# A two-layer graph, state-space and expert-mixture kernel: where the counts, the chunk ends and the routing steps stand, how the second mixture is split, and how many buffers its gathers rotate through

## The chip, the cores and the metric

The kernel runs on one core of a Trainium2 chip. The metric is device time in microseconds (us) of one execution. Five engines each work through their own queue in order: TensorE (PE, with its weight loads shown as PEld), VectorE (DVE), ScalarE (ACT), GpSimd (POOL) and SyncE (SP, which here only issues DMAs). Plain DMAs are issued by SP. Indirect DMAs (gathers and scatters by a list of row numbers) are issued by POOL.

## The reference, cut to what matters

Two layers over 4096 tokens of 256 features. `adj` is 4096 x 4096 and sparse (each row holds about eight non-zero values besides its diagonal).

```
# layer 0
x = x + L0_gnn(layernorm(x), adj)      # relu(adj @ x @ gcn_w + gcn_b), layernorm, then a
                                       # selective scan (state 16, inner 512) along the tokens
x = x + L0_ffn(layernorm(x))           # 8 experts, top 2, gelu, hidden 512
# layer 1
x = x + L1_gnn(layernorm(x), adj, adj)
x = x + L1_ffn(layernorm(x))           # 6 experts, top 2, three 256x256 matrices each

def L1_gnn(h, adj, simlar):
    sim  = tanh(adj * simlar)
    filt = sim * (adj > 0)
    vals, idx = top_k(filt, 700)       # all of a row, if it has at most 700 entries
    nnz  = sum(filt != 0, axis=1)
    keep = arange(700) < nnz
    new_adj = zeros.at[rows, idx].set(where(keep, vals, 0))
    h2 = tanh(h @ W_proj + b_proj)
    return relu(new_adj @ (h2 @ W_gcn) + b_gcn)

def L1_ffn(f):
    rh = relu(f @ router_w1 + router_b1)
    p  = softmax(rh @ router_w2 + router_b2); top_w, top_i = top_k(p, 2)
    w  = softmax(top_w)
    return sum over the two chosen experts of w * expert(f)
```

## The kernel before, in words

Tokens are worked in 8 chunks of 512 (`CW`, `NC`); a chunk is 4 tiles of 128 rows (`TPC`). The stages follow one another in one program:

1. **Lead-in** (to the first scan). Eight layer norms of `x` into `gn` (outside any order written by hand), then inside `tc.manual_schedule`, where the order of the code is the order on PE, DVE, ACT and POOL, the generator `propagation(0)` (L832): for each half chunk of 256 columns it streams 8 tiles `at` of `adjT` (128 x 4 x 256, three buffers, loaded by SP) and multiplies them with `gn`. One half takes 33 `advance` steps. In between, the neighbour lists of the listed chunks (2, 4, 6) begin: `lists.pair(q)` (L528) loads two row blocks of `adj` in eight pieces, finds the eight largest of each 512 columns on DVE (L562, L563), and four more pieces sort and pack them. The first list's twelve pieces (`EARLY_LISTS`) stand on DVE before the chunk's bias `L909`, with which the chain to the first scan begins.
2. **Scan** of layer 0, eight chunks of 32 steps, paced by DVE.
3. **First mixture** (8 experts) in tiles of 256 rows, `expert_tiles` (L666), with the rest of the lists beside it.
4. **Features**: `Features` (L1721) for each chunk combines the expert outputs (`yg`), norms, transposes, projects and writes the rows of `gnd` that gathers read. Its tiles and those of the later routing rotate through `WORK` buffers of tag `fm`.
5. **Neighbour loop** (L1863 to L1890), also in an order written by hand, SP included. It has 80 iterations: the five dense chunks (0, 1, 3, 5, 7) by 16 tiles of `adjT`. Iteration `k` does, in this order: `source(k+3)` (three ACT passes over the tile, and on DVE the count of positive entries, L1814 or L1817), `fetch(k+5)` (SP), the running `Route.prepare` generators one step each, the running `table`, `taken.upto(int(PACE*(k-2)))`, and `product(k)`: eight matrix products on PE, shown as sixteen records of L1825. After a chunk's last product, `finish` (L1830) closes it: a count product on PE, its maximum, bias, relu and residual on DVE. A load waits until ACT and DVE are done with the tile that had its buffer (`AHEAD + 1` buffers), a source until PE is done with the `f` that had its buffer (`LEAD + 1`), so PE can be only some six iterations ahead of DVE.
   The listed chunks are not multiplied. `Listed` (L1667) has 216 slots (6 pairs of tiles by 36); for each, POOL gathers 128 rows of `gnd` into one of ten ring buffers (L1681), and DVE adds them, scaled, into `x3` (L1697), in the order of the slots; a buffer is gathered into again when DVE has used it. Six of the buffers are tiles of their own, four are the rows of `x3` of the last chunk, which must be given up (`retire`) six iterations before the end.
   `ROUTES` says at which iteration a finished chunk starts its routing for the second mixture (`Route.prepare`, L637): layer norm on DVE (with `rsqrt`, L93, by four Newton steps), four transposes per half on PE (L144), a hidden layer (L197), logits (L654), top-2 choice (`router`, L147), placing (`place`, L269) and one-hot rows (`one_hot`, L319). `Part.tables` (L343) turns the choices of the first `SPLIT` chunks into row lists for POOL and expert numbers for SP, in groups of 8 columns: DVE, ACT, then PE (L419).
6. **Second mixture**, in two lots of tiles: 27 for the first six chunks (`few[0]`), 11 for the last two. Beside the first lot's tiles, `also` (L1953) advances the routing and table of the remaining chunks; beside the second lot's, `to_out` combines the first lot's chunks and stores them. The last two chunks are combined at the very end. `combine` (L729) reads with three `yg` buffers, two of which one chunk needs.

A program prints the functions that the change touches:

## Time and profile before

Three runs of the kernel before took 2341.86, 2342.48 and 2334.57 us. The profiled execution took 2333.76 us, of which its span, from the first to the last instruction, is 2332.0. The stages, cut at the first scan, the first and last product of the neighbour loop, the first expert product of the second mixture and the last bias of its two lots:

| stage | from | to | length us | PE busy | DVE busy | POOL busy |
|---|---|---|---|---|---|---|
| lead-in | 0 | 147.8 | 147.8 | 134.1 | 88.9 | 14.2 |
| scan | 147.8 | 1245.0 | 1097.2 | 1035.9 | 1054.7 | 817.1 |
| first mixture | 1245.0 | 1559.0 | 314.0 | 280.2 | 197.4 | 141.4 |
| features | 1559.0 | 1662.7 | 103.7 | 77.0 | 51.9 | 11.3 |
| neighbour loop | 1662.7 | 2052.7 | 390.0 | 324.3 | 313.4 | 277.1 |
| to the second mixture | 2052.7 | 2059.5 | 6.8 | 2.5 | 6.6 | 4.6 |
| second mixture, first lot | 2059.5 | 2232.0 | 172.5 | 171.6 | 67.3 | 105.2 |
| second lot | 2232.0 | 2310.7 | 78.7 | 68.2 | 33.2 | 33.8 |
| last stores | 2310.7 | 2332.0 | 21.3 | 0.0 | 6.7 | 1.9 |

How to read it: times within a row overlap, since the engines work side by side. Where one engine's busy time comes near the length of the stage, it sets the stage's length; where none does, waits between engines do, and they have to be read from the views of waits and from the order of time. A gather's own time on POOL (about 1.3 us) is that of issuing it; the rows land later.

### The profile page before, as it was taken

To read this page: it belongs to the slowest core of one execution; us is meant where nothing else is said; L and a number is where in the kernel's file an instruction comes from. 1 tells how busy PE (TensorE), PEld (TensorE's weight loads), DVE (VectorE), ACT (ScalarE), POOL (GpSimd) and SP (SyncE) were. 2 spreads that over 40 slices of the span, in tenths; PEclk is the share of its full clock that TensorE was granted. 3 is DMA by queue.
4 is the path that set the end of the run, shared out by engine and by line. 5 is a ranking of instruction groups with operands and counts; after the bars stand their busy time and mean duration, and the time that the engine had idled before them with its cause. 6 is when DMAs were issued, how large, how long until landed. Compare 5 with 4: busy or idle time off the path is not lost. (4 is left out here: it accounts for less than half of the span.)

```text
span 2332.0 us, 28125 instructions
## 1 busy us (share of the span) xinstructions
PE 2093.7 (90%) x8229; PEld 1498.5 (64%) x8229; DVE 1820.0 (78%) x3229; ACT 1196.5 (51%) x2064; POOL 1406.7 (60%) x1054
## 2 busy tenths in 40 slices
PE   8999999999999999997896999968978978799995
PEld 7666665656666565654564787855767766677874
DVE  4869999999999999999997997125377988864243
ACT  4256657465665746567673324214667765623321
POOL 1047777787877778776763454521387676746652
PEclk9999999999999999998897999988989998899998
DMA  8579899999989999998975999743455454367896
GB/s 293 169 207 247 229 282 239 271 248 250 268 231 283 241 269 249 252 263 240 278 262 170 300 366 317 231 145 118 153 152 169 148 168 136 108 206 219 248 293 214
DMA packets 302677, 532.29 MB, mean 228 GB/s; under 512 B 31323, under 2 KB 170575, under 8 KB 301616
## 3 DMA queue, kind: packets, MB, share of 16 engines
q1 hardware_dynamic: 244720, 416.84, 55.9%
q0 software_dynamic: 57792, 113.54, 21.8%
q8 instruction: 69, 1.13, 0.2%
q14 instruction: 96, 0.79, 0.1%
HBM read 434.34 MB, written 49.02 MB: 207 GB/s over the span
## 5 line engine op out<-in xcount | busy, mean ns | idle before, releaser
L1315 POOL TENSOR_TENSOR db<-du,bb 128x1024 f32<-128x1024 f32 x256 | 607.2, 2372 | 311.1 <-DVE hc L1348 74.3
L1338 DVE TENSOR_TENSOR_SCAN db<-da,state,db 128x512 f32<-128x512 f32 x512 | 627.3, 1266 | 19.9 <-ACT da L1331 17.7
L844 PE MATMUL pt<-at,gn 128*128 128x256 f32 x2048 | 478.3, 386 | 14.3 <-ACT gn L129 9.0
L844 PEld LDWEIGHTS pt<-at,gn 128*128 128x128 f32 x2048 | 396.5, 194 | 135.2 <-issue 63.8
L1331 ACT ACTIVATE da<-dt,negA 128x512 f32<-128x512 f32 x512 | 346.1, 688 | 245.7 <-DVE db L1338 235.9
L1348 DVE TENSOR_TENSOR hc<-db,cb 128x1024 f32<-128x1024 f32 x256 | 328.0, 1281 | 18.2 <-issue 0.9
L1365 PE MATMUL psy<-hc,ident 128*128 128x512 f32 x560 | 291.9, 615 | 3.4 <-DMA hc<-hc 3.4
L1825 PE MATMUL pf<-gn,f 128*128 128x256 f32 x1280 | 293.9, 391 | 0.0
L1825 PEld LDWEIGHTS pf<-gn,f 128*128 128x128 f32 x1280 | 250.4, 197 | 38.8 <-issue 3.3
L1681 POOL DMA_INDIRECT ring<-gnd,ls_idx x134 | 172.2, 1285 | 91.0 <-DVE x L1697 41.5
L690 PE MATMUL ps_h<-xkT,wk 128*128 128x256 f32 x864 | 214.4, 390 | 13.3 <-DVE xkT L715 12.1
L675 PE MATMUL ps_y<-wk,hk 128*128 128x256 f32 x864 | 214.0, 384 | 0.3
L680 DVE TENSOR_TENSOR yk<-ps_y,bk 128x512 f32<-128x512 f32 x73 | 50.2, 687 | 199.0 <-PE ps_y L675 161.0
L1352 POOL DMA_DIRECT2D hc<-hc x232 | 201.9, 870 | 0.2
L690 PEld LDWEIGHTS ps_h<-xkT,wk 128*128 128x128 f32 x864 | 159.1, 193 | 51.4 <-DVE xkT L715 19.0
L675 PEld LDWEIGHTS ps_y<-wk,hk 128*128 128x128 f32 x864 | 162.0, 192 | 22.1 <-ACT hk L694 1.6
L1365 PEld LDWEIGHTS psy<-hc,ident 128*128 128x128 f32 x560 | 105.2, 194 | 84.0 <-issue 60.1
L960 PE MATMUL ps_xz<-hT,w_in 128*128 128x512 f32 x256 | 117.0, 600 | 14.1 <-ACT hT L944 7.5
L694 ACT ACTIVATE hk<-ps_h,d0r_b 128x256 f32<-128x256 f32 x104 | 48.9, 474 | 136.1 <-PE ps_h L690 136.1
L1809 ACT ACTIVATE f<-at 128x1024 f32<-128x1024 f32 x80 | 84.4, 1055 | 64.6 <-PE pf L1825 56.9
L1681 POOL DMA_INDIRECT x<-gnd,ls_idx x82 | 101.3, 1235 | 27.0 <-issue 11.9
L694 ACT ACTIVATE hk<-ps_h,d1ap_b 128x256 f32<-128x256 f32 x108 | 51.2, 474 | 128.0 <-PE ps_h L690 127.9
(392 smaller groups left out, 3067.9 us busy)
## 6 DMA issues: line engine op xcount, KB each, us to landing
at<-in_adjT_dram SPq DMA_DIRECT2D x208, 512.0 KB, 4.7
bb<-bcd SPq DMA_DIRECT2D x128, 512.0 KB, 5.6
cb<-bcd SPq DMA_DIRECT2D x128, 512.0 KB, 5.3
hc<-hc POOLq DMA_DIRECT2D x232, 256.0 KB, 6.3
wk<-in_L_ffn_W_dram SPq DMA_DIRECT2D x70, 512.0 KB, 5.8
wk<-in_L_ffn_expert_w_dram SPq DMA_DIRECT2D x114, 256.0 KB, 4.3
ls_at<-in_adj_dram SPq DMA_DIRECT2D x32, 512.0 KB, 8.4
hc<-in_adj_dram SPq DMA_DIRECT2D x16, 512.0 KB, 5.2
```

The lines of the kernel that those rows point to most:

```text
L675: nc.tensor.matmul(ps[:, j, :], hT[:, m, j * P:(j + 1) * P], w[:, m, :], start=(m == 0), stop=(m == kb_out - 1),)
L690: nc.tensor.matmul(ps[:, j, :], w[:, d, m * P:(m + 1) * P], xT[:, d, :], start=(d == 0), stop=(d == DB - 1),)
L844: nc.tensor.matmul(pt[:, k, :], xl[:, j, k * P:(k + 1) * P], at[:, jj, :], start=(j == 0 and k == 0), stop=(j == NT - 1 and k == DB - 1),)
L960: nc.tensor.matmul(ps, w_in[:, k, m * P:(m + 1) * P], self.hT[:, k, :], start=(k == 0), stop=(k == DB - 1),)
L1315: nc.gpsimd.tensor_tensor(self.db, self.f.du[self.half][:, self.mi:self.mi + 1, :].to_broadcast([P, 2, CW]), self.bb, ALU.mult,)
L1331: nc.scalar.activation(da, self.f.dt[self.half][:, self.mi, :], AF.Exp, scale=negA[:, self.m, n:n + 1])
L1338: nc.vector.tensor_tensor_scan(self.db[:, j, :], da, self.db[:, j, :], state[:, self.m, n:n + 1], ALU.mult, ALU.add,)
L1348: nc.vector.tensor_tensor(self.hc, self.db, self.cb, ALU.mult)
L1352: nc.gpsimd.dma_start(self.hc[:, 0, :], self.hc[:, 1, :], accum_op=ALU.add)
L1365: nc.tensor.matmul(f.psy[m], ident, self.hc[:, j, :], start=False, stop=(self.g == GS - 1 and j == last),)
L1681: nc.gpsimd.indirect_dma_start(out=to[:, :], out_offset=None, in_=gnd[:, :], in_offset=bass.IndirectOffsetOnAxis(ap=lists.idx[:, q, s:s + ...
L1825: nc.tensor.matmul(pf[:, t, :], f[:, jj, t * P:(t + 1) * P], gn[:, j, :], start=(j == 0 and t % 2 == 0), stop=(j == NT - 1 and t % 2 == 1),)
```

## The change

It has six parts, all but the last two of which reorder or move work.

- The count of chunk 0 is made in the lead-in, from the tiles `at` that `propagation(0)` loads anyway, with a count product on PE and two maxima on DVE for each half; the loop's `source` and `finish` leave it out for chunk 0. The pieces of the first list now alternate with the second half's steps.
- `finish` runs at the start of the next iteration; the count product stays at the chunk's end (`total`).
- The layer norm of a routing yields between its statistics and its root and has one more empty step before the transposes; placing is two steps; the table's PE products run one step after the DVE work they read.
- `SPLIT` 5 instead of 6: the first lot is 23 tiles for five chunks, the second 15 tiles for three, 38 in all as before. The table of the first lot starts at iteration 69 with one step each instead of 75 with two.
- The ring has twelve buffers (four of its own, the four rows of the last chunk, and the four of the last listed chunk, the latter until slot 132), then eight; all 216 slots are done inside the loop at `PACE` 2.85.
- `rsqrt` makes three Newton steps instead of four. `WORK` is 8.

```diff
-SPLIT = 6
+SPLIT = 5
-RING = 10
-WORK = 7
+RING = 4
+WORK = 8
-PACE = 2.8
-RETIRE = 6
-ROUTES = {17: 0, 29: 2, 33: 1, 49: 3, 55: 4, 64: 5}
-TABLES = 75
-SPARE = 2
+PACE = 2.85
+ROUTES = {17: 0, 29: 2, 33: 1, 49: 3, 55: 4}
+TABLES = 69
...
-        for i in range(4):
+        for i in range(3):
...
         if alone:
+            yield
             rsqrt(rs, mv[:, :, 1])
...
             nc.tensor.matmul(
                 tot[:, :(G + 1) * E], ones, oh.rearrange("p g e -> p e g"), start=True, stop=True
             )
+            yield
...
+            last = None
+            def add():
+                if last is not None:
+                    g0, eq = last
+                    for g in range(S):
+                        nc.tensor.matmul(
+                            ps[:, :2 * C], dp.lo[:, g0 + g, :], eq[:, :2, g, :],
+                            start=(g0 + g == 0), stop=(g0 + g == NG - 1),
+                        )
...
-                for g in range(S):
-                    nc.tensor.matmul(
...
+                add()
+                last = (g0, eq)
                 yield
+            add()
+            yield
...
-            for _ in layernorm_parts(self.source[:, c * TPC:(c + 1) * TPC, :], xn, alone=True):
+            norm = layernorm_parts(self.source[:, c * TPC:(c + 1) * TPC, :], xn, alone=True)
+            next(norm)
+            yield
+            for _ in norm:
                 pass
+            yield
             yield
...
-        def propagation(c):
+        def propagation(c, count=False):
...
                     at = ats.pop(0) if ats else adjacency(r0, j4)
+                    if count and j4 == 0:
+                        cnt = w2p.tile([P, 4, HW], BF16, name="cnt0", tag="db")
+                        nc.vector.tensor_scalar(cnt, at, 0.0, None, ALU.is_gt)
+                    elif count:
+                        nc.vector.scalar_tensor_tensor(cnt, at, 0.0, cnt, ALU.is_gt, ALU.add)
...
+                if count:
+                    pc = ps_y.tile([P, CW], F32, name="psy", tag="psy")
+                    for jj in range(4):
+                        nc.tensor.matmul(
+                            pc[:1, :HW], ones[:, :1], cnt[:, jj, :], start=(jj == 0), stop=(jj == 3)
+                        )
+                    h = (r0 // HW) % 2
+                    nc.vector.tensor_reduce(chalf[:, h:h + 1], pc[:1, :HW], AX.X, ALU.max)
...
-            advance(NT + 1)
-            fr.do_gcn(1)
             made = [lists.pair(q, w2p, "hc", 6, 3) for q in range(EARLY_PAIRS)]
             made = itertools.chain(*made)
-            for _ in range(EARLY_LISTS):
+            for _ in range(NT // 4):
+                advance(4)
+                next(made)
+            advance(1)
+            fr.do_gcn(1)
+            for _ in range(EARLY_LISTS - NT // 4):
                 next(made)
...
-        ring = [keep1.tile([P, D], F32, name=f"ring{i}") for i in range(RING - TPC)]
-        tail_ring = [x3[:, NT - TPC + t, :] for t in range(TPC)]
+        ring = [keep1.tile([P, D], F32, name=f"ring{i}") for i in range(RING)]
+        early_ring = [x3[:, t, :] for t in lists.tiles[-TPC:]]
+        ring += [x3[:, NT - TPC + t, :] for t in range(TPC)]
...
+                self.last = len(self.slots) - TPC // 2 * PAIR - 12
             def fetch(self):
+                if self.next >= self.last:
+                    self.free = [f for f in self.free if any(f is r for r in ring)]
...
-            if j2 == 0:
+            if c == 0:
+                pass
+            elif j2 == 0:
...
+                if ended is not None and k % H2 == 0:
+                    finish(*ended)
+                    ended = None
                 if k in ROUTES:
...
                 if k >= TABLES:
-                    for _ in range(2):
-                        next(table, None)
-                if k == len(seq) - RETIRE:
-                    taken.retire()
+                    next(table, None)
                 taken.upto(int(PACE * (k - 2)))
-                if k == len(seq) - 1 and taken.left():
-                    taken.upto(max(taken.left()) + 1)
                 product(k, pf)
                 if j2 == H2 - 1:
-                    finish(c, pf)
-        assert not routes
+                    ended = (c, pf, total(c) if c else None)
+            finish(*ended)
+        assert not routes and taken.done == len(taken.slots)
...
         def routing():
             for b in range(NC - SPLIT - 1, -1, -1):
-                while b == 0 and taken.done < len(taken.slots):
-                    yield
                 for n, _ in enumerate(late.prepare(b)):
-                    if n % 6 == 5:
+                    if n in (5, 9):
                         yield
                 yield
...
         def also(n):
-            taken.upto(taken.done + SPARE)
```

In the built program, the order on DVE in the lead-in shows where the counts fall: the first three of the first half stand between the statistics of chunks 1, 2 and 3 and the step that asks POOL for their roots, the next two among the last chunk's statistics, and in the second half one count precedes each of the eight list pieces, with the half's maximum ahead of the list's last four pieces. On SP, four of the list's loads now stand ahead of the second half's second tile, where before its first three tiles stood ahead of them.

More of the change, by code (lines that the diff above doesn't have):

```diff
@@ L76 @@
     cmax = const.tile([1, NC], F32, name="cmax")
+    chalf = const.tile([1, 2], F32, name="chalf")
     x1d = [dram.tile([CW, D], F32, name=f"x1d{c}") for c in range(NC)]
@@ L106, in rsqrt @@
             nc.vector.scalar_tensor_tensor(t, t, -0.5, y, ALU.mult, ALU.mult)
-            nc.vector.scalar_tensor_tensor(rs if i == 3 else y, t, 1.5, y, ALU.add, ALU.mult)
+            nc.vector.scalar_tensor_tensor(rs if i == 2 else y, t, 1.5, y, ALU.add, ALU.mult)
     def layernorm_parts(src, dst, scalar=False, alone=False):
@@ L267, in choose_parts, with place, place_parts @@
             )
-        def place(self, b, psum, tag, pool):
+        def place(self, *args):
+            for _ in self.place_parts(*args):
+                pass
+        def place_parts(self, b, psum, tag, pool):
             E, G, g0 = self.E, 2 * self.T[b], 2 * self.t0[b]
@@ L417, in tables @@
                 )
-                for g in range(S):
-                    nc.tensor.matmul(
-                        ps[:, :2 * C], dp.lo[:, g0 + g, :], eq[:, :2, g, :],
-                        start=(g0 + g == 0), stop=(g0 + g == NG - 1),
-                    )
+                add()
+                last = (g0, eq)
                 yield
+            add()
+            yield
             inv = tp.tile([P, 2, C], F32, name="tb_inv", bufs=1)
@@ L660, in prepare @@
             yield from dp.choose_parts(b, logits, self.bias_b, True, small)
+            place = dp.place_parts(b, self.psum, self.tags[2], small)
+            next(place)
             yield
-            dp.place(b, self.psum, self.tags[2], small)
+            for _ in place:
+                pass
             yield
@@ L851, in propagation @@
                 halves.append(pts)
+                if count:
[6 more added lines that the diff above has]
+                    nc.vector.tensor_reduce(chalf[:, h:h + 1], pc[:1, :HW], AX.X, ALU.max)
+                    if h == 1:
+                        nc.vector.tensor_tensor(
+                            cmax[:, c:c + 1], chalf[:, :1], chalf[:, 1:], ALU.max
+                        )
                 yield True
@@ L1403, in advance @@
                 return k
-            prop = propagation(0)
+            prop = propagation(0, True)
             advance(NT + 1)
@@ L1661 @@
         gnd = dram.tile([N, D], F32, name="gnd")
-        for t in ring + tail_ring:
+        for t in ring + early_ring:
             nc.gpsimd.memset(t, 0.0)
@@ L1672, in __init__ @@
                 self.slots = [(q, s) for q in range(lists.n) for s in range(PAIR)]
-                self.free, self.at, self.next, self.done = ring + tail_ring, {}, 0, 0
-                self.keep = True
+                self.free, self.at, self.next, self.done = early_ring + ring, {}, 0, 0
+                self.last = len(self.slots) - TPC // 2 * PAIR - 12
             def fetch(self):
+                if self.next >= self.last:
+                    self.free = [f for f in self.free if any(f is r for r in ring)]
                 while self.free and self.next < len(self.slots):
@@ L1707, in upto @@
                     self.done += 1
-                    if self.keep or any(buf is r for r in ring):
-                        self.free.append(buf)
+                    self.free.append(buf)
                     self.fetch()
-            def retire(self):
-                self.keep = False
-                self.free = [f for f in self.free if any(f is r for r in ring)]
-            def left(self):
-                return [g for g, f in self.at.items() if not any(f is r for r in ring)]
         taken = Listed()
@@ L1811, in source @@
             nc.scalar.activation(f, f, AF.Tanh)
-            if j2 == 0:
+            if c == 0:
+                pass
+            elif j2 == 0:
                 cnt = cnts[c] = tb.tile([P, 2, CW], BF16, name="cnt", bufs=2)
@@ L1828, in product, with total @@
                     )
-        def finish(c, pf):
+        def total(c):
             pc = ps_m.tile([P, CW], F32, name="pc", tag="m")
@@ L1834, in finish @@
                 nc.tensor.matmul(pc[:1], ones[:, :1], cnt[:, jj, :], start=(jj == 0), stop=(jj == 1))
-            nc.vector.tensor_reduce(cmax[:, c:c + 1], pc[:1], AX.X, ALU.max)
+            return pc
+        def finish(c, pf, pc):
+            if pc is not None:
+                nc.vector.tensor_reduce(cmax[:, c:c + 1], pc[:1], AX.X, ALU.max)
             rows = slice(c * TPC, (c + 1) * TPC)
@@ L1852 @@
         )
-        routes = {}
+        routes, ended = {}, None
         with tc.manual_schedule(engines={
```

## The prediction

> **What bounds the kernel now.** I read the windows by stage first, then PE's waits in the stage that the change concerns, then that stage in order of time, then its gathers, and last the two places where the change adds work: the lead-in and the end. The scan is DVE's (1054.7 of 1097.2 us) and the change doesn't touch it. In the neighbour loop, 390.0 us long, no engine is full:
>
> ```profile
> 1662.70:2052.70 390.00, 324.33 (x1470) 273.30 (x1469) 313.44 (x801) 260.76 (x269) 277.12 (x220) 0.91 0.50 151
> ...
> 2059.50:2232.00 172.50, 171.59 (x824) 140.18 (x825) 67.29 (x232) 57.28 (x122) 105.15 (x108) 0.99 0.78 235
> ```
>
> Columns: window, length, then busy time and count of PE, PEld, DVE, ACT and POOL, clock, DMA. The loop's PE has 324 us of work, DVE 313, POOL 277; the second line, the second mixture's first lot, is full on PE. What PE waits for, loop and transition:
>
> ```profile
> PE ps_tr L144 <- DVE xn_r L134: 51.1, 6, 14.8
> PE pf L419 <- ACT tb_eq L413: 14.6, 2, 10.7
> ...
> PE ps_xt L711 <- DVE cmax L1899: 4.3, 1, 4.3
> ```
>
> The six routings cost 51.1 us of waiting for their norms, the table 14.6. Nothing else holds PE up. But this tells who was late, not why. In order of time:
>
> ```profile
> 1718.53 7.17 PE L1825 MATMUL pf<-gn,f 128*128 128x256 f32 x32
> 1740.54 2.42 PE L144 MATMUL ps_tr<-ident,xn_r 128*128 128x128 f32 x8 [14.84 <-DVE xn_r L134]
> 1742.75 5.02 PE L1825 MATMUL pf<-gn,f 128*128 128x256 f32 x16
> ...
> 1749.32 3.62 PE L1825 MATMUL pf<-gn,f 128*128 128x256 f32 x16
> ```
>
> An iteration of PE starts 3.45 us after the last while nothing holds it (32 records take 7.17); after a long wait the next 16 take 5.02, not 3.62, at a granted clock of 0.57 in that stretch. PE reached the first routing 18 iterations in, while DVE still waited for gathers. They are POOL's:
>
> ```profile
> L1681 POOL DMA_INDIRECT ring<-gnd,ls_idx x134 | 172.2, 1285 | 91.0 <-DVE x L1697 41.5 <-DMA gnd<-gn 21.3 <-issue 16.8
> L1681 POOL DMA_INDIRECT x<-gnd,ls_idx x82 | 101.3, 1235 | 27.0 <-issue 11.9 <-DVE x L1697 7.8 <-DVE d1a_oh L175 1.8
> ...
> 1692.69 1.22 DVE L1817 SCALAR_TENSOR_TENSOR cnt<-at,cnt 128x1024 bf16<-128x1024 f32 x1
> ...
> 1692.88 1.90 POOL L1681 DMA_INDIRECT x<-gnd,ls_idx  x1 [0.30 <-DVE x L1697]
> ...
> 1699.10 1.00 POOL L1681 DMA_INDIRECT ring<-gnd,ls_idx  x1 [0.30 <-DVE x L1697]
> ```
>
> 216 gathers took 172.2 + 101.3 = 273.5 us. Each also has 0.30 us before it, whatever happens: 64.8. That is 338 us, 1.57 each. Idle beyond that, without the first wait of 21.3, is 91.0 + 27.0 - 21.3 - 64.8 = 31.9. From 1667.8 this gives 2038, and the last indeed starts at 2036.9. An iteration takes 2.8 slots, so POOL alone asks 4.4 us for it against PE's 3.45. **So the loop is paced by gathers, and PE's waits are where it meets that pace.**
>
> **The change, part by part.**
>
> *Neighbour loop.* DVE loses the counts of chunk 0 (0.70 + 15 x 1.22 = 19.0), one routing (norm 6.5, choice 4.3, placing 2.9, one-hot 1.2: 14.9, summed from its rows), a Newton step in five routings (5 x 3 x 0.165 = 2.5) and a sixth of the table (2.5): 39 of 313. PE loses one routing (transposes, hidden layer and logits, 5.2 us). POOL's 216 gathers all stay. Fifteen fewer counts may each free the 0.4 us by which a gather beside one is longer (gathers beside one last around 1.4, alone 1.00): -6. The 31.9 us of extra idle stand at routings and chunk ends, 12 of them between 1787 and 1827 (19 gathers in 40 us), where DVE waits for products or exponentials that are only just issued. With those steps apart, DVE lighter and twelve buffers until slot 132, I take 24 of the 32 as gone. The last gather then ends at about 2038 - 30 = 2008. What hangs on it: DVE adds it (landing 3 us, two additions, 1.0), closes the last chunk (0.7 + 2 x 0.7 + 1.2 = 3.3); POOL gathers the first expert rows (2 x 1.3, landing 3.6); PE transposes and DVE copies (2). First expert product about 11 us behind: 2019, where now it is 2059.5. The table no longer decides, as it ends at iteration 77. **-40.** Bounds: if the idle doesn't shrink and only the counts help, the last gather ends at 2032 and the gain is 16; if all idle goes and gathers fall to 1.15, 216 x 1.45 from 1667.8 ends at 1981 and the product starts at 1992, -67, which PE just allows (1662.7 + 80 x 3.45 + 5 routings at 8 = 1979).
>
> [...]
>
> *Lead-in, added.* Sixteen counts on DVE, 19 us, and eight small PE products. The chain to the first scan starts from DVE:
>
> ```profile
> 46.24 0.69 DVE L562 MAX8 hc<-hc 128x8 f32<-128x512 f32 x1 [4.75 <-DMA hc<-in_adj_dram]
> ...
> 71.46 1.99 PE L902 MATMUL ps_gcn<-gcn_w,pts 128*128 128x256 f32 x8 [0.68 <-ACT pts L850]
> ...
> 77.08 1.28 DVE L909 TENSOR_TENSOR h<-ps_gcn,gcn_b 128x512 f32<-128x512 f32 x2
> ```
>
> PE's product was ready at 73.5, the bias waited for twelve list pieces: eight of 2.79 us (4 x 0.68 and loads) and four, 8.5 us. With counts a piece takes 4.0 us. In its favour, the list's first loads go out some 4 us earlier (one tile ahead of them, not three). First half: counts 2 and 3 stand before a root (2 x 1.2), hidden by the 3 to 5 us that norms are ahead of PE; count 4 holds its tile from 26.1 to about 29.4, so a later load is late and PE by 2 to 3.5. Then pieces from 42 to 74, the half's maximum 75, the rest of the list 84: the bias at about 83.8. **+6.5** (bounds +2, if tiles aren't held, and +13, if the loads come no earlier either). All of the scan moves with it.
>
> *Features.* One more `fm` buffer. The loads of `yg` stand behind the store of `gnd` on SP and wait for that, not for a buffer, but for 0.6 us every second chunk: **-0.5** (0 to -3).
>
> *First lot.* A third routing, and a table of three groups, not two, go beside tiles that fill PE. Undisturbed tiles end 6.04 or 5.21 us apart, 5.87 on average; the eight from 2080.8 to 2137.8, with two routings and the table, take 57.0, 10 more than 8 x 5.87. **+5**, half of that (+3 to +9).
>
> *Second lot.* 38 tiles as before. Its eleven took 78.7 us, 14 above 11 x 5.87, with the six combined chunks whose loads and stores stand before the next weights on SP. Five instead of six: **-2** (0 to -3).
>
> *End.* Three chunks to combine, not two, with three `yg` buffers:
>
> ```profile
> 2314.77 6.56 SPq L738 DMA_DIRECT2D yg<-d1b_ys  x6
> 2318.59 1.67 DVE L745 SCALAR_TENSOR_TENSOR oc<-yg,d1b_wv,x 128x256 f32<-128x256 f32 x4 [3.80 <-DMA yg<-d1b_ys]
> ...
> 2324.53 1.67 DVE L745 SCALAR_TENSOR_TENSOR oc<-yg,d1b_wv,oc 128x256 f32<-128x256 f32 x4
> ```
>
> The third chunk's second load needs a buffer that DVE frees at 2326.2. Load 3.5, eight additions 3.3, store 3.3, and the 2.8 from the last landing to the end: 2339.5. **+7.5** (+4, if loads overlap, to +10).
>
> Sum: 6.5 - 0.5 - 40 + 5 - 2 + 7.5 = -23.5. From the profiled execution's 2333.8 this gives 2310. That execution lies 8 us under the median of the three runs (2341.9), which spread from 2334.6 to 2342.5; I add half of the distance: **2314 us**.
>
> **The rivals.**
>
> *Gathers no longer bind* (PE or DVE does, first product at about 1995, -64 instead of -40): 2290. For it: gathers last 1.00 with DVE quiet. Against: the list additions, which lengthen most gathers, all stay.
>
> *The idle only moves.* DVE's additions keep their bursts, after slot 132 eight buffers serve where ten did, and 22 to 32 us of idle stay: loop -16 to -24, and with +16.5 elsewhere 0 to -7.5. Time 2334. For it: 41.5 us of ring idle were ended by DVE's additions.
>
> *Eight buffers throttle the second half: slower.* From slot 132 to the last, before, 84 gathers took 151 us (1.79 each) with ten buffers or six. If the round trip of a buffer sets the pace, eight make it 2.24. Gather 132 starts at 1667.8 + 132 x 1.55 = 1872, the last ends at 2060, the first expert product is at 2071, 11.5 later than now. With +16.5 elsewhere: +28, 2366. It decides from a pace of 1.90, at which the whole change gives nothing, and is slower by 0.5% from 2.04. Against: a buffer's trip is 1.3 + 3 landing + at most one iteration of 4.4 and a closing chunk, some 10 to 12 us, and 8 x 1.57 = 12.6 just covers it.
>
> **How the numbers follow.** Measurements of this kernel tell about 0.5% (12 us) from no change. Forecast 0.58, nearly all of it faster; gathers don't bind 0.14; the idle moves 0.17, of which 0.03 is faster; throttled 0.11, of which 0.02 is within 0.5%. Faster 0.74, same 0.17, slower 0.09. The range 2284 to 2342 takes in the forecast's bounds, most of the second case and half of the first. The forecast's own is 2298 to 2330.
>
> **What will show it.** The 16-record groups of L1825 should start some 4 us apart nearly throughout, with PE's waits for `xn_r` under 15 us in all and none for `tb_eq` over 4; the last L1681 should start near 2007 plus the lead-in's shift of 6.5, with extra idle under 12; the chunk's bias in the lead-in should start near 84, the first scan near 154; the first lot's early tiles should be slower for three routings; from last bias to the end some 29 us. It is wrong if the last gather ends as late as now, if the bias in the lead-in is at 77 or at 90, or if the pace of gathers beyond slot 132 is over 1.8.

## The result and the profile after

Six runs of each kernel on one chip: 2306.9 us median after (2304.8 to 2309.1), 2334.6 before (2333.8 to 2342.5). The ratio is 0.9871, with a 95% interval of 0.9854 to 0.9888: 27.7 us faster. The profiled execution took 2307.5 us, its span is 2305.6. Cut where the stages were cut before, in us:

| stage | before | after | difference | predicted |
|---|---|---|---|---|
| lead-in, to the first scan | 147.8 | 158.7 | +10.9 | +6.5 |
| scan, first mixture, features | 1514.9 | 1514.7 | -0.2 | -0.5 |
| neighbour loop, and on to the first expert product | 396.8 | 347.4 | -49.4 | -40 |
| both lots of the second mixture, 38 tiles | 251.2 | 255.3 | +4.1 | +3 |
| from the last bias to the end | 21.3 | 29.5 | +8.2 | +7.5 |
| sum | 2332.0 | 2305.6 | -26.4 | -23.5 |

The time lies 7 us under the 2314 that were predicted, well inside the range, and each stage went in the direction that was said. Two terms are mis-sized, the loop's and the lead-in's, and the loop's reason, as the experiments show, was not the right one.

The windows of the lead-in and of the loop (length, busy time of PE, PEld, DVE, ACT and POOL, granted clock, DMA):

```profile
0.00:158.67 158.67, 139.25 (x542) 104.58 (x543) 106.67 (x321) 54.14 (x97) 14.21 (x26) 0.97 0.63 206
...
1673.35:2013.60 340.25, 312.66 (x1438) 264.89 (x1437) 286.31 (x721) 257.61 (x263) 263.54 (x219) 0.95 0.57 171
```

In the loop PE is now busy for 312.7 of 340 us, where it was 324.3 of 390. What it waits for there and in the transition:

```profile
PE ps_tr L144 <- DVE xn_r L134: 13.1, 4, 5.9
PE pf L417 <- ACT tb_eq L429: 9.4, 2, 9.1
PE ps_pl L285 <- DVE d1a_oh L177: 4.5, 2, 3.3
...
PE ps_xt L733 <- DVE cmax L1941: 1.5, 1, 1.5
```

The norms' 51.1 us have become 13.1, the table's 14.6 have become 9.4, and nearly all of that is one wait. The waits of the placing (`ps_pl`), 4.5 us, did not stand among the waits before. In order of time, at the first routing and at the table:

```profile
1745.07 2.37 PE L144 MATMUL ps_tr<-ident,xn_r 128*128 128x128 f32 x8 [2.49 <-DVE xn_r L134]
1747.23 4.75 PE L1864 MATMUL pf<-gn,f 128*128 128x256 f32 x16
...
1977.91 0.82 PE L417 MATMUL pf<-tb_eq,d_lo 128*128 128x100 bf16 x8 [9.13 <-ACT tb_eq L429]
1978.53 5.21 PE L1864 MATMUL pf<-gn,f 128*128 128x256 f32 x16
```

The first routing stops PE for 2.49 us, not 14.84. The sixteen records behind a stop still take 4.75 or 5.21 us instead of 3.62. The gathers:

```profile
L1726 POOL DMA_INDIRECT x<-gnd,ls_idx x128 | 151.2, 1181 | 60.6 <-DMA gnd<-gn 21.2 <-issue 12.8 <-DVE x L1742 11.3
L1726 POOL DMA_INDIRECT ring<-gnd,ls_idx x88 | 109.2, 1241 | 31.3 <-DVE x L1742 12.7 <-issue 9.8 <-DVE cnt L1856 2.1
```

They take 260.4 us (273.5 before). Idle beyond the 0.30 of each and the first wait of 21.2 is 60.6 + 31.3 - 21.2 - 64.8 = 5.9 us (31.9 before). From slot 132 on, with eight buffers, they follow each other every 1.65 us, from start to start (1.82 before, counted the same way). The last one starts at 2008.5. In the lead-in, one wait of DVE's counts, the bias and PE's next step of the chain to the scan:

```profile
49.68 1.22 DVE L866 SCALAR_TENSOR_TENSOR cnt<-at,cnt 128x1024 bf16<-128x1024 f32 x1 [2.45 <-DMA at<-in_adjT_dram]
...
86.04 1.28 DVE L948 TENSOR_TENSOR h<-ps_gcn,gcn_b 128x512 f32<-128x512 f32 x2
...
91.97 2.80 PE L976 MATMUL ps_turn<-ident,h 128*128 128x128 f32 x8 [5.73 <-ACT h L968]
```

The bias starts at 86.04 instead of 77.08, and PE, which had its own product ready at 78.5, now stops 5.73 us for what follows from it. At the end, the loads and the last additions:

```profile
2280.16 6.68 SPq L760 DMA_DIRECT2D yg<-d1b_ys  x6
...
2297.47 1.67 DVE L767 SCALAR_TENSOR_TENSOR oc<-yg,d1b_wv,oc 128x256 f32<-128x256 f32 x4 [1.62 <-DMA yg<-d1b_ys]
```

### The profile page after: what moved, and what is told of

It is laid out like the page before. It is cut to its first block, busy times and chain, and to the rows that moved or that the text cites. A ratio compares the mean times of both kernels' runs of the same rounds, so it can differ in the third digit from the quotient of the medians.

```text
span 2305.6 us, 28092 instructions
## 1 busy us (share of the span) xinstructions
PE 2087.7 (91%) x8235; PEld 1492.4 (65%) x8235; DVE 1813.0 (79%) x3207; ACT 1196.3 (52%) x2064; POOL 1397.9 (61%) x1056
## 5 line engine op out<-in xcount | busy, mean ns | idle before, releaser
L1864 PE MATMUL pf<-gn,f 128*128 128x256 f32 x1280 | 289.2, 387 | 0.0
L712 PEld LDWEIGHTS ps_h<-xkT,wk 128*128 128x128 f32 x864 | 160.5, 195 | 49.5 <-ACT hk L716 14.6
L1726 POOL DMA_INDIRECT x<-gnd,ls_idx x128 | 151.2, 1181 | 60.6 <-DMA gnd<-gn 21.2
L697 PEld LDWEIGHTS ps_y<-wk,hk 128*128 128x128 f32 x864 | 160.5, 190 | 21.3 <-ACT hk L716 1.4
L1404 PEld LDWEIGHTS psy<-hc,ident 128*128 128x128 f32 x560 | 105.4, 195 | 84.8 <-issue 60.6
L1726 POOL DMA_INDIRECT ring<-gnd,ls_idx x88 | 109.2, 1241 | 31.3 <-DVE x L1742 12.7
L1016 PE MATMUL ps_xz<-xc,dK 128*128 128x512 f32 x256 | 114.8, 592 | 0.0
L1846 ACT ACTIVATE f<-at 128x1024 f32<-128x1024 f32 x80 | 84.4, 1055 | 51.1 <-PE pf L1864 39.2
```

What stands on the lines that cost most here:

```text
L697: nc.tensor.matmul(ps[:, j, :], hT[:, m, j * P:(j + 1) * P], w[:, m, :], start=(m == 0), stop=(m == kb_out - 1),)
L712: nc.tensor.matmul(ps[:, j, :], w[:, d, m * P:(m + 1) * P], xT[:, d, :], start=(d == 0), stop=(d == DB - 1),)
L1404: nc.tensor.matmul(f.psy[m], ident, self.hc[:, j, :], start=False, stop=(self.g == GS - 1 and j == last),)
L1726: nc.gpsimd.indirect_dma_start(out=to[:, :], out_offset=None, in_=gnd[:, :], in_offset=bass.IndirectOffsetOnAxis(ap=lists.idx[:, q, s:s + ...
L1864: nc.tensor.matmul(pf[:, t, :], f[:, jj, t * P:(t + 1) * P], gn[:, j, :], start=(j == 0 and t % 2 == 0), stop=(j == NT - 1 and t % 2 == 1),)
```

## The experiments

Every kernel but one is the changed kernel, altered in one part or, in the last, in three; the other is the kernel before with fewer gathers. "Extra idle" is POOL's between gathers, beyond 0.30 each and the first wait. The ratio is to the kernel before, timed on the same chip, which gave 2336.5 us (first four rows of experiments), 2332.0 (next four), 2335.2 (next three) and 2361.9 (the last). Kernels timed on different chips are best compared by this ratio, in which 0.0010 is 2.3 us. The other columns are those of the one profiled execution.

| kernel | median us | ratio, 95% interval | first scan | loop | extra idle | last gather ends |
|---|---|---|---|---|---|---|
| before | 2334.6 | 1 | 147.8 | 390.0 | 31.9 | 2037.9 |
| after | 2306.9 | 0.9871, 0.9854 to 0.9888 | 158.7 | 340.2 | 5.9 | 2009.5 |
| counts back in the loop | 2300.9 | 0.9846, 0.9822 to 0.9870 | 150.0 | 343.2 | 5.9 | 2009.2 |
| all steps together | 2350.6 | 1.0069, 1.0042 to 1.0096 | 157.8 | 383.7 | 30.4 | 2040.6 |
| eight buffers | 2315.0 | 0.9919, 0.9888 to 0.9950 | 157.2 | 342.9 | 7.1 | 2011.1 |
| split at six | 2318.8 | 0.9928, 0.9905 to 0.9951 | 158.9 | 361.9 | 12.8 | 2018.3 |
| chunk ends at once | 2304.4 | 0.9876, 0.9842 to 0.9909 | 158.9 | 338.9 | 3.8 | 2007.3 |
| routing at once | 2324.1 | 0.9962, 0.9947 to 0.9977 | 158.6 | 356.6 | 14.4 | 2030.5 |
| after, 180 gathers | 2291.7 | 0.9816, 0.9793 to 0.9840 | 159.5 | 329.3 | 27.6 | 1995.3 |
| loads ahead, five buffers | 2300.9 | 0.9853, 0.9828 to 0.9878 | 159.5 | 339.9 | 7.1 | 2013.1 |
| before, 180 gathers | 2326.8 | 0.9962, 0.9944 to 0.9980 | 149.8 | 379.0 | 67.9 | 2032.4 |
| table at once | 2334.7 | 0.9990, 0.9973 to 1.0007 | 158.0 | 365.4 | 15.3 | 2028.5 |
| lists behind the bias | 2299.8 | 0.9849, 0.9818 to 0.9881 | 149.6 | 339.7 | 5.9 | 2003.3 |
| three edits combined | 2368.0 | 1.0033, 1.0011 to 1.0056 | 148.0 | 366.3 | 31.7 | 2032.1 |

**Do gathers pace the loop?** The central claim of the prediction, tried on the kernel before.

```
+                    if s % 6 == 5:
+                        self.at[self.next] = None
+                        self.next += 1
+                        continue
                     to = self.at[self.next] = self.free.pop(0)
...
-                    buf = self.at.pop(g)
+                    given = self.at.pop(g)
+                    buf = b_gcn_b if given is None else given
```

> The kernel before, with every sixth gather left out (180 instead of 216); the additions of those slots add a constant row, so DVE's work stays, and the rows of the listed chunks come out otherwise. The prediction said that gathers pace the neighbour loop of the kernel before (390 us) and that PE's waits are where it meets that pace. Theory G (that is so): 36 x 1.57 = 56 us less on POOL; the loop falls until PE's work and the sixth routing and table stop it, 340 to 355 us, kernel -35 to -50 us. Rival P (the routing's and the table's waits set the loop, each stalling PE while DVE does a whole norm, and POOL only follows): loop within 8 us of 390. In between (both near the bound, as the same cut in the changed kernel gave 10.9 us of 54): 365 to 380.

With some 56 us of POOL's work gone, the loop fell by 11.0 us and the kernel by 8.5. The window of the loop and two stops of PE in it, those of the first and the last routing:

```profile
1669.20:2048.16 378.96, 322.66 (x1470) 272.32 (x1469) 312.62 (x801) 260.79 (x269) 239.91 (x184) 0.93 0.49 149
```

```profile
1739.14 2.42 PE L144 MATMUL ps_tr<-ident,xn_r 128*128 128x128 f32 x8 [6.90 <-DVE xn_r L134]
...
1969.53 2.21 PE L144 MATMUL ps_tr<-ident,xn_r 128*128 128x128 f32 x8 [10.39 <-DVE xn_r L134]
```

POOL's extra idle is 67.9 us now, and the last gather ends only 12 us earlier against the loop's start. The first stop shrank from 14.84 to 6.90; there DVE had been waiting for the first gathers (21.4 us in the kernel before, from 1665 to 1741). The others are nearly as long as they were. The time from the start of the iteration before to the start of the iteration named, in us:

```
iteration        18     30     34     50     56     65     75     76
before        20.66  11.66  10.73  14.83  10.97  16.21  15.01  10.34
180 gathers   12.72  11.51  10.73  13.76  10.90  16.05  15.01  10.21
```

In both kernels 54 of the 79 distances are under 3.7 us, and in them PE's records follow one another without idle time. The loop before the change thus ran at PE's own pace but for 25 iterations: of the 113.8 us by which its distances exceed 3.45 each, 101.6 stand in 14 distances of over 6 us, at stops or right behind one. Of these stops only the first hung on gathers for more than about 1 us. Theory G's 340 to 355 falls. With 379.0 the loop ends at the edge of what was called in between (365 to 380), 3 us outside rival P's bound: rival P but for the first stop, which gives 7.9 of the 11.0 us.

**The same cut in the changed kernel.**

> The changed kernel with every sixth gather left out (180 gathers instead of 216); the additions of those slots add a constant row instead, so DVE has the same work, and the rows of the listed chunks come out otherwise. POOL has 1.206 + 0.30 us a gather now, 331 of the loop's 340 us. Theory G (POOL's gathers still set the loop's length): 36 x 1.5 = 54 us less on POOL, the loop falls until PE stops it (80 x 3.45 + 5 routings of 8 = 316, or somewhat more with its remaining waits): loop 316 to 326, kernel -14 to -24 us. Rival P (PE, DVE and their waits set the loop now, POOL is only nearly full): loop within 4 us of 340. Rival D (DVE's 288 additions and counts pace it): likewise within 4 us, with DVE waiting less for gathers but busy throughout.

The loop fell by 10.9 us, to 329.3, where theory G wanted 316 to 326 and rival P 340: between the two. The kernel's ratio fell by 0.0055, some 13 us, just short of the 14 that theory G wanted at least.

```profile
1676.43:2005.78 329.35, 309.88 (x1438) 263.03 (x1437) 285.88 (x721) 257.27 (x263) 240.24 (x188) 0.97 0.56 172
```

PE is busy for 310 of 329 us. The distances at iterations 20, 32 and 52, each with a stop in it, went from 8.26, 12.14 and 9.80 to 4.33, 7.34 and 7.93; the table's, at 71, stayed (13.37 and 13.25). After the change gathers still lengthen the remaining stops at routings, by 0.2 us for each microsecond taken off POOL, the same share as before the change.

**All steps together, then one kind at a time.** First norm, placing, chunk ends and the table's products all as before the change (and with them the steps in which the second mixture takes its late routings):

```
-            yield
             rsqrt(rs, mv[:, :, 1])
...
-            next(norm)
-            yield
             for _ in norm:
                 pass
-            yield
             yield
...
-                add()
                 last = (g0, eq)
+                add()
                 yield
-            add()
-            yield
...
-            place = dp.place_parts(b, self.psum, self.tags[2], small)
-            next(place)
             yield
-            for _ in place:
-                pass
+            dp.place(b, self.psum, self.tags[2], small)
...
-                    ended = (c, pf, total(c) if c else None)
+                    finish(c, pf, total(c) if c else None)
```

> The changed kernel with one part undone: layer norm, placing, chunk end and the table's products stand in one step again, as before the change (the placing keeps its halves, run one right behind the other). Theory G (what counts is the extra idle before gathers, 5.9 us now, 31.9 before the change; apart steps remove idle because DVE no longer stands waiting with additions behind it): PE waits for xn_r return to over 35 us, extra idle of gathers rises to 18 to 25, loop +12 to +19, kernel 2319 to 2326. Rival P (the waits of PE for the norms set the loop): five norms with 8.5 us each and the table's 14.6 come back in full, +40 us or more, 2347. Rival C (counts and buffers made the loop's gain, the steps none): within 4 us of the changed kernel.

The loop grew by 43.5 us, nearly all that the change had gained there; this is rival P's number. PE's waits:

```profile
PE ps_tr L143 <- DVE xn_r L133: 34.2, 5, 11.8
PE pf L416 <- ACT tb_eq L428: 27.5, 5, 12.1
```

The extra idle of the gathers came back as well, 30.4 us, though POOL had nothing else to do than in the changed kernel. In the two kernels with 180 gathers it is 67.9 and 27.6 us. The idle time follows mostly from what holds DVE and PE; cutting gathers adds to it.

Chunk ends alone (only the last two lines of the diff above and the call of `finish` behind it):

> The changed kernel with only the chunk's end undone: bias, relu and residual follow the chunk's last product in its own iteration again, so that DVE waits there for products only just issued. With all steps undone the loop grew by 43.5 us, of which the idle of gathers is 24.6. Theory G (each step that DVE waits on holds additions, and so gathers, up): five ends, each holding DVE by some 2 to 3 us more: extra idle 6 -> 14 to 20, loop +8 to +15. Rival R (the routing and table steps make all of it): loop within 3 us of 340. Rival E (the ends make most of it): loop +25 or more.

Loop 338.9, kernel 2304.4: no effect that can be told. Rival R holds. Routing alone (statistics, norm and placing):

> The changed kernel with only the routing undone: statistics, root and norm of a routing in one step, the transposes one step earlier, placing in one step; chunk ends and table as in the changed kernel. Theory G: DVE does a whole norm (6.5 us) in one stretch and waits in placing for a product just issued; additions stand behind it; extra idle 6 -> 15 to 22, PE waits for xn_r from 13 to over 30, loop +15 to +25. Rival E (the chunk ends make most of the 43.5): loop within 8 us of 340. Rival T (the table's products make it): loop within 8 us, in this run and in the one with only the chunk ends undone.

Loop +16.4, PE's waits for `xn_r` 33.7 us (13.1), extra idle 14.4 (5.9): about the sizes that theory G gave, which rival P of the run before gives too, so this run does not tell them apart. The table alone:

> The changed kernel with only the table's products undone: each group's products on PE stand in the step of the DVE and ACT work that they read. All steps undone cost the loop 43.5 us, routing alone 16.4, chunk ends alone -1.3. If the parts add, the table makes the remaining 28: PE's waits for tb_eq go from 9 to over 25 us, loop +18 to +28, kernel 2325 to 2335. Rival J (the parts need each other: with the routing undone the table starts late and meets the loop's end, by itself it costs little): tb_eq waits below 20, loop below +10.

Loop +25.1, as was said if the parts add: PE's waits at the table are 24.1 us for `tb_eq` and 3.8 more put down to a DVE addition, where rival J wanted less than 20 and a loop below +10. The three parts, 16.4 + 25.1 - 1.3 = 40.2, nearly add up to the 43.5. The table's first three groups:

```profile
1983.69 0.82 PE L417 MATMUL pf<-tb_eq,d_lo 128*128 128x100 bf16 x8 [12.60 <-ACT tb_eq L429]
1984.31 5.31 PE L1862 MATMUL pf<-gn,f 128*128 128x256 f32 x16
1993.46 0.52 PE L417 MATMUL pf<-tb_eq,d_lo 128*128 128x100 bf16 x8 [3.84 <-ACT tb_eq L429]
1993.82 5.37 PE L1862 MATMUL pf<-gn,f 128*128 128x256 f32 x16
2003.02 0.82 PE L417 MATMUL pf<-tb_eq,d_lo 128*128 128x100 bf16 x8 [3.84 <-DVE x L1740]
```

Groups come about 10 us apart, where an undisturbed iteration is 3.45. PE reaches each group's products before DVE and ACT have made what they read; the next iteration's records then run at 5.3 us, and the next group finds PE waiting again. One step apart, only the first group stops it.

**The counts of chunk 0 back in the loop**, and the lead-in's former order.

```
-            prop = propagation(0, True)
+            prop = propagation(0)
...
-            if c == 0:
-                pass
-            elif j2 == 0:
+            if j2 == 0:
```

> The changed kernel with one part undone: chunk 0 is counted in the neighbour loop again, and the lead-in has its former order (both halves, then the twelve list pieces). Theory G (POOL's gathers pace the loop, a count costs the loop only what it lengthens a gather and the idle it causes): the bias of the lead-in starts at 77 instead of 86, the first scan at 148 instead of 159 (-11), the 15 counts after the first lengthen gathers by 0.4 us each (+6) and idle grows by 2 to 4, so the loop grows by 8 to 10: -1 to -3 us against the changed kernel. Rival D (DVE's work paces the loop): all 19.0 us of counts come back in the loop, 2307 - 11 + 19 = +8 us. Rival N (the loop has slack there): the loop stays 340 us and the kernel gains the whole lead-in, -11 us.

The bias starts at 78.0 and the first scan at 150.0, 8.7 us earlier; the loop grew by 3.0, the gathers' time by 2.7 (263.2), the extra idle not at all. 19.0 us of DVE work thus cost the loop 3: not the 19 of rival D, less than the 8 to 10 of theory G and more than rival N's nothing. The stages between took 5.7 us more in this one profile, though nothing in them differs; the median is 6.0 us lower, as -8.7 and +3.0 give, and the two intervals overlap. By the two stages, moving these counts together with the list's new order was a loss of 5.7 us; the medians alone don't show it.

**Four list pieces behind the bias.**

```
-EARLY_LISTS = 12
+EARLY_LISTS = 8
```

> The changed kernel with eight list pieces ahead of the chunk's bias in the lead-in instead of twelve; the other four (8.5 us of DVE) follow with the second list's pieces, behind the statistics. Theory B (the bias waits for DVE, and the lead-in's 10.9 us are DVE's counts ahead of it, PE's wait for the turn and the low clock that follows it): bias at 77.5 instead of 86, PE's wait for ps_turn from 5.7 to below 3, first scan 4 to 8 us earlier, kernel -4 to -8 us. Rival W (PE's own order paces the lead-in, which is busy 141 of its 159 us): bias at 77.5 all the same, first scan within 2 us of 158.7, kernel within 2 us. Rival L (the four pieces are late behind the bias): first scan later than 160.

```profile
77.53 0.67 DVE L948 TENSOR_TENSOR h<-ps_gcn,gcn_b 128x512 f32<-128x512 f32 x1
```

```profile
86.03 1.04 PE L976 MATMUL ps_turn<-ident,h 128*128 128x128 f32 x8
```

The wait of 5.73 us is gone, the turn takes 1.04 us instead of 2.80, and the first scan starts at 149.6: 9.1 of the 10.9 us are back, with the counts still in the lead-in. What is left, 1.8 us, is no more than profiles with the same lead-in differ: the first scan of the kernel before starts at 147.8 and, with fewer gathers, at 149.8; that of the changed kernel and of the runs that leave its lead-in alone at 157.2 to 159.5. The bias came 8.5 us earlier, which is what the four pieces take on DVE. So theory B is right about what the bias waits for, and its 4 to 8 us are a little exceeded; the low clock behind PE's wait (0.77 from 90 to 105 us) had little part in it, as the account of the lead-in below shows. Moving four pieces behind the bias of the kernel before, which waited for DVE as well (PE ready at 73.5, the bias at 77.1), was not tried. Of the kernels that do the whole computation this one has the lowest median, 2299.8 us, and by the ratio (0.9849) it is level with the counts back in the loop (0.9846); its interval overlaps that of the changed kernel, so the gain is read from the stage.

**Eight buffers from the start.**

```
-        early_ring = [x3[:, t, :] for t in lists.tiles[-TPC:]]
+        early_ring = []
```

> The changed kernel without the four early buffers: eight buffers for all 216 gathers. From slot 132 on, where it has eight anyway, the changed kernel makes a gather every 1.65 us, before that every 1.47. Theory G (a buffer's trip of 10 to 12 us is just covered by eight): the first 132 slots take 0 to 0.1 us more each, 0 to +13 us, I take +5. Rival T (the trip of a buffer sets the pace with eight): the first 132 slots go at 1.65 or slower, +24 us and more; with the 2.24 of the scaled trip +100.

Loop +2.7, extra idle +1.1. The median, 2315.0, comes from runs that spread from 2307.4 to 2321.9, and its interval only touches the changed kernel's; the profiled one took 2307.9, so the slower ones left no trace that tells why. Rival T's +24 us fails on every run: the trip of a buffer does not set the pace. In the profiled execution the four early buffers bring 2.7 us; in the median the kernel without them is 8 us slower, and the cause of the difference is open.

**Six chunks in the first lot.**

```
-SPLIT = 5
+SPLIT = 6
-ROUTES = {17: 0, 29: 2, 33: 1, 49: 3, 55: 4}
-TABLES = 69
+ROUTES = {17: 0, 29: 2, 33: 1, 49: 3, 55: 4, 64: 5}
+TABLES = 75
...
-                    next(table, None)
+                    for _ in range(2):
+                        next(table, None)
```

> The changed kernel with the split undone: six chunks in the first lot, a sixth routing in the loop from iteration 64, the table from 75 on with two steps each (and seven buffers of tag fm, as the sixth chunk's rows take that room). Theory G (the end pays for the third chunk, the loop gains little by the split, since gathers pace it): the end is 8 us shorter (21 instead of 29.5), the first lot 5 shorter, the second 2 longer, the loop and transition longer by the sixth routing's share: PE 5.2 us and gathers held up by 3 to 8, transition 4: together 0 to +6 us, 2307 to 2313. Rival S (the split made much of the loop's gain, as the sixth routing and its table stand at the end of the loop where nothing covers them): loop and transition +30, less the 11 at the end: 2326 or more.

The loop is 21.7 us longer, with 16.3 us of waits for `tb_eq` and 19.0 for `xn_r`; from the last bias to the last addition the end is 7.4 shorter (15.7 against 23.1), the tiles take 2.9 less. The median is 11.9 us above the changed kernel, about midway between the theories. Loop and transition together are 20.5 us longer, so the split gains twice the 10.3 that it costs.

**Loads of the last combinations a tile ahead.**

```
-        yg = [pool.tile([P, TPC, D], F32, name="yg", **(tag or {"bufs": 3})) for _ in range(2)]
+        yg = [pool.tile([P, TPC, D], F32, name="yg", **(tag or {"bufs": 5})) for _ in range(2)]
...
+                while going:
+                    next(going.pop(), None)
                 if (n - few[0]) % 3 != 0 and ready:
-                    stores.append(to_out(dp1[0], ready.pop(0), op[0]))
+                    going.append(to_out(dp1[0], ready.pop(0), op[0]))
+                    next(going[0])
```

> The changed kernel with the last combinations altered: a chunk's two loads are issued one tile ahead of the additions that read them, five buffers for these loads instead of three, the sums written in place, and the last chunk stored in two parts. In the changed kernel the second lot has three slow tiles (11.25, 8.74 and 10.20 us where 6.04 is usual), in which DVE waits 5.27 us for a load just issued and PE's next copy stands behind it. Theory A (a load issued a step ahead takes the wait away): the three tiles lose 8 to 12 us together; the end, where the third chunk's second load waited for a buffer, loses 2 to 4: -10 to -16 us. Rival Q (what holds the tile up is the loads and stores ahead of the next weights on SP): the slow tiles stay, only the end gains: -2 to -4 us.

```profile
2189.22 0.48 DVE L769 SCALAR_TENSOR_TENSOR x<-yg,d1a_wv,x 128x256 f32<-128x256 f32 x1 [5.00 <-DMA yg<-d1a_ys]
```

The end is 3.9 us shorter (19.2), as both theories said; the second lot's slow tiles stayed (12.28, 10.00 and 8.24 us). But the wait itself was not tried: the loads were issued at 2185.1 and the first addition stood on DVE 4.1 us later, as in the changed kernel (2184.7 and 2188.7). This part has no order written by hand, and putting the load earlier in the code did not put the addition later on DVE.

**Three edits combined**: the lists behind the bias, five buffers with the last chunk in two parts, and the table's products two steps behind.

```
-EARLY_LISTS = 12
+EARLY_LISTS = 8
...
-            def add():
-                if last is not None:
-                    g0, eq = last
+            def add(most):
+                if len(last) > most:
+                    g0, eq = last.pop(0)
```

> The changed kernel with three edits that the runs so far speak for: eight list pieces ahead of the lead-in's bias (by itself 2299.8 us, -7), five buffers for the last combinations' loads with the sums written in place and the last chunk stored in two parts (the end 19.2 instead of 23.1 us from the last bias to the last addition, -4), and the first lot's table products two steps behind their DVE work instead of one (PE still waits 9.1 us there, once, in iteration 71). If the stops of PE set the loop and one more step hides most of the last: 9.1 -> below 5, loop 340 -> 335, kernel 2290 to 2295. If that wait is one for DVE's backlog, and not for a step too early, it moves with the products: loop 339 to 342, kernel 2295 to 2298.

It was timed on a chip on which the kernel before took 2361.9 us (2347.7 to 2368.6), some 26 more than elsewhere, and was 0.3% slower than that, so neither forecast came. The profiled execution, 2346.1 us, is the fastest of its twelve, 22 us under their median. In its profile one iteration of the loop took 36.1 us, its records 2.1 to 2.8 us apart, with a kind of PE wait that none of the other profiles shows, one in which PE waits for nothing that the profile names:

```profile
PE pf L1865 <- issue: 28.8, 20, 2.2
...
PE pf L417 <- ACT tb_eq L429: 3.5, 4, 1.7
```

The table's wait did fall from 9.1 to 1.7 at the longest, and without the 32.7 us by which that iteration exceeds the usual one the loop would be 333.6. But the long iteration also let the other engines catch up (the stop at iteration 20 is missing behind it), so 333.6 is no measurement. The two lots took 266.7 us, 11.4 more than in the changed kernel, so the loop is not the only slow part of this profile. Whether the long iteration belongs to this kernel or to that chip is open, and so is whether the combination is faster.

## Why the prediction held, and where its reasons did not

**What bounds the loop.** "So the loop is paced by gathers, and PE's waits are where it meets that pace" is the step that failed. Cutting a sixth of the gathers took 11.0 us off the 390, not 35 or more, and nearly 8 of them at the first stop. The loop is PE's own 80 iterations of 3.45 us, 276 us, and the rest, 114 us before and 64 after, is stops, the routing's products and the slower records behind a stop (5.02 us for sixteen before, 4.75 and 5.21 after, instead of 3.62). The stops stand where PE reads what DVE and ACT were only then told to make: norms and hot rows of the table. Putting those reads back beside what they read, with the same work on every engine, cost the loop 43.5 us. How much of a stop is that step's own work and how much is DVE's backlog was not separated. The lines shown with the prediction could not settle it. Distances of 3.45 us right up to a stop look like PE's own pace, but PE may be some six iterations ahead: a loop held to POOL's 4.4 us an iteration falls behind PE by 0.95 us in each, so PE could run some 28 iterations (6 x 4.4 / 0.95, an estimate from these numbers) before it is held, and the longest stretch between two stops is 18. Only taking gathers away told the two apart. POOL's 338 us were added up to nearly the loop's length and its idle time was taken for a cause, though its releaser was DVE. That the sum met the last gather was no evidence either: the additions are tied to the iterations by `PACE`, so the last gather comes near the loop's end whatever sets the pace.

Of the signs that were named, the groups some 4 us apart throughout did not come (54 of 79 distances are under 3.7 in the changed kernel as before), nor did the table's waits of at most 4 us (one is 9.1) or the first scan near 154 (158.7). The waits for `xn_r` (13.1, under 15), the extra idle (5.9, under 12), the pace behind slot 132 (1.65, under 1.8) and the end (29.5 for some 29) came as said; the last gather started at 2008.5, 5 us before the time named.

**The loop's -40.** It came out at -49.4. That the steps apart are what helps was among its reasons, but each part was priced by what it saved the gathers, so that the number lies within its bounds is in part luck: the gathers ended earlier because the stops went, not the other way round. Undone one by one, routing is worth 16.4 us, the table 25.1, the split 21.7, the counts 3.0, the buffers 2.7, the chunk ends nothing; the sum, 68.9, exceeds the 49.8 that the loop lost, so the parts overlap. That the table's step matters less where the table has more time, as with the split, would explain it but was not tried. The Newton step, `PACE` and the retiring of buffers were not undone by themselves. The prediction gave the counts 6 us (measured 2.7 of gathers' time), and the table and the split no number of their own beyond "the table no longer decides". The last gather ended 39 us earlier against the loop's start, not 30 (the gathers' own time fell by 13.0 us, where 6 were said, the extra idle by 26.0, where 24 were), and the first expert product followed 11.3 us behind it, where 11 were said.

Which of DVE's work lengthens a gather was read from what overlaps it. Counts after a chunk's first and list additions both read two tiles; in the changed kernel a gather that overlaps such a count by more than 0.3 us took 1.50 us on average (74 of them), one that so overlaps list additions and no count 1.09 (73), and one beside which DVE does nothing 1.01 (10). So the prediction's "the list additions, which lengthen most gathers" was a misreading: beside a count a gather took some 0.5 us longer, beside additions less than 0.1.

**The lead-in's +6.5.** It came out at +10.9. The bias was 2.2 us later than the 83.8 worked out (the pieces began at 44.3, not 42, and counts waited for tiles, 2.45 us once). The prediction moved the first scan with the bias; the distance between them grew from 70.7 to 72.6 us. That PE had to stop for the bias and ran slower afterwards (2.80 us for the turn, 1.04 without the stop) is not shown to be the cause: over all the profiles the distance lies between 70.7 and 72.7, with 72.0 where the wait of 5.73 us is gone and 72.4 in the kernel before with fewer gathers, whose lead-in is untouched. So these last 1.9 us are no more than such profiles differ. That all twelve list pieces had to lie ahead of the bias was no necessity, as the run with four of them behind it shows; the counts stayed ahead of it in that run.

**Lots and end.** +4.1 for +3 and +8.2 for +7.5: the three combinations, three buffers and their order were read rightly from the lines of before, and the run with five buffers gives 3.9 of it back.

**The rivals.** The throttled second half needed a pace of 1.90 us from slot 132 on; it was 1.65, and eight buffers from the start cost the loop 2.7 us. That the idle only moves was wrong, as it fell to 5.9. "Gathers no longer bind" is near to what the kernel is after the change, but its price of -64 came from the same wrong start, that they had bound before.

## What to carry to other kernels

Before a queue is called the pace-setter, take a part of its work away: if the loop gets shorter by a fifth of what was taken, as here (11.0 of 56 us), the queue mostly follows, and its idle time is a consequence. Distances at the bound engine's own pace between its stops are a hint of this, but where buffers let that engine run ahead they do not prove it. In an order written by hand, what an engine reads should be issued a step earlier on the engine that makes it; here that alone was worth over 40 us. Work that is moved into another stage can stand ahead of the chain of that stage, as the counts do here (first scan at 158.7 with them in the lead-in, 150.0 without); look for other work there that can go behind the chain in its place, as four list pieces did (149.6).

## What the runs showed of the hardware

Three stops of PE in the changed kernel cost more than their length. After the 9.13 us at the table the next sixteen records took 5.21 us instead of 3.62, with a granted clock of 0.50 from 1971.4 to 1981.6, and after the 2.49 us at the first routing 4.75, with a granted clock of 0.50 from 1746.1 to 1749.5: 1.6 us lost behind the one and 1.1 behind the other. In the lead-in the granted clock was 0.77 from 90 to 105 us, behind the wait of 5.73; the turn took 2.80 us and the sixteen records behind it 5.06, and without that wait 1.04 and 3.62. With the same 1438 records in the loop, PE was busy for 322.0 us with all steps together (granted clock 0.92) and for 312.7 in the changed kernel (0.95). How this cost depends on the length of a stop was not tried.

The median of the kernel before was 2332.0 to 2336.5 us in four of the comparisons and 2361.9 in the fifth, on another chip. That is one such comparison, and why it was slower is open.
